# Two-layer cross attention: layer 2's image scores copied out of the score tile and sent through DRAM, in place of a product of their own

## The chip, the cores and the metric

The kernel runs on one core of a Trainium2 chip. The metric is the device time of one execution in microseconds (us); the median of several runs stands for a kernel. Beside the runs there is one profiled execution with its trace. Engines are named as in the profile: PE (TensorE matmuls), PEld (its weight loads), DVE (VectorE), ACT (ScalarE), POOL (GpSimd) and SP (SyncE, which issues most of the transfers here).

## What is computed

Two layers of cross attention with an image adapter, on 4096 tokens: x is 16 x 256 x 320, the context 16 x 256 x 512, with 20 heads of 16. The last 4 of the 256 context tokens of a batch are image tokens. Layer 2, the one that the change touches, cut to what matters (the output product and the residual follow):

```python
text_ehs, ip_ehs = encoder_hidden_states[:, :-4], encoder_hidden_states[:, -4:]
q, k_t, v_t = heads(hidden_states @ W_q), heads(text_ehs @ W_k), heads(text_ehs @ W_v)
probs_t = softmax(einsum('bhsd,bhtd->bhst', q, k_t) * attn_scale)
text_out = einsum('bhst,bhtd->bhsd', probs_t, v_t)
k_ip, v_ip = heads(ip_ehs @ W_k_ip), heads(ip_ehs @ W_v_ip)
attn_scores = einsum('bhsd,bhnd->bhsn', q, k_ip) * attn_scale
qsem = l2norm(einsum('bhst,bte->bhse', probs_t, text_ehs))
sem = einsum('bhse,bne->bhsn', qsem, l2norm(ip_ehs))
probs_ip = softmax(attn_scores + 0.5 * sem) * spatial_mask
out = text_out + einsum('bhsn,bhnd->bhsd', probs_ip, v_ip)
```

`attn_scores`, the scores of every query against the four image keys, are what the change gets in another way.

## The kernel before

The work is cut into slots: one slot is four heads (a group g of five) of one batch b. Slots 0 to 79 are layer 1, slots 80 to 159 layer 2, and two more drain the pipeline. Products that need full accuracy are made of rounded halves (a high and a low part). Queries, keys and activations are kept in DRAM (`qd`, `kd`, `x1d`) and come back as stacks (`qs`, `ks`) whose rows are the halves and, in layer 2, two rows with the row maxima.

A layer-2 slot k has two halves, t = 0 and 1, and each half of the tokens is one call of `both1` (L761). It issues, in this order:

- 4 matmuls into `T` (L775): transposed scores of slot k, already shifted by the row maxima;
- 4 matmuls into `S` (L780): plain scores of slot k + 2, 128 queries by 4 heads by 256 keys. S is one PSUM tile of two banks and has no second buffer. Its last four columns of each head (T1:S in the code) are the scores against the image keys; before, nothing reads them;
- DVE's maximum over the first 252 columns (L781), into `mn`;
- in the half t = 0, `attend1` of slot k - 2: 32 matmuls (L825, L828) into `P`;
- ACT's two exps of T into the tile P (L788).

Between the halves stand the other steps of the slot: `rounded1` (ACT's `ctb`, L806, and POOL's rest, L807), `norm1` of the slot before (L816 matmuls with the matrix `gm` into one X bank, four or three blocks, then DVE's multiply `wt`, L817, which frees the bank), and `maxima1` (L794: two small matmuls that turn `mn` into rows in an X bank, ACT's copy `mt`, L796, and a transfer from ACT's queue into `qs`). There are three X banks, used in turn by everything that isn't S, T or P. Fillers run at the thirds of a slot, from a table of due times: the next batch's keys (`kst`, `kd`), tokens (`gm`, `v1t`, `cta`), queries (L517 to L537), the image softmax (L881), and the batch's end (L931 the image output, L932 its add into `hT`, L754 the output rows `xc`).

The next batch's queries are `open1` (L942). After `queries` it calls `image1` (L502), two DVE multiplies (L506) which spread the four image keys over 128 columns with the mask `kmask`; nine matmuls (L205) of queries by these, into an X bank; and a DVE transpose (L955) into `si`, 128 x 8 x 32, the layout of the image softmax: the token in partitions and free dimension, then group and image key. The image softmax reads `si` on POOL (L899), one batch after.

PE's instructions keep the order of the program text. In the main loop the order of DVE, ACT, POOL and SP is chosen by the compiler's scheduler from its own timeline; `anchor` marks an instruction for others to be queued behind. SP issues the transfers in its order, and an issue that has to wait holds back those behind it.

Of the kernel before, what the change touches and what calls it, by code (L numbers as in the profile page):

```python
# [8 lines left out]
F32 = mybir.dt.float32  # L9
FR = mybir.dt.float32r  # L10
# [7 lines left out]
S = 256  # L18
# [6 lines left out]
NIP = 4  # L25
BI = B * NIP
T1 = S - NIP
# [21 lines left out]
def xattn2(  # L49
# [234 lines left out]

    rn = const_tile([128, BI], "rn")
    kip = const_tile([128, 2, 3, BI], "kip", FR)
    kmask = const_tile([128, 3, 32], "kmask")


    def keys_out(d, m, kst, b=slice(None)):  # L290
# [119 lines left out]
    def weights6():  # L410
        cip = w1["cip"]
        w1["v"] = yield from weights(wv1_d, "wC", None, 0.3, "rawc")
        wvi1 = yield from weights_by_column(wvi1_d, 0.3, "rawc")
        vip = buf("rawc", [128, 512], bufs=2, name="vip")[:BI, :CP]
        for m in range(3):
            ms = slice(m * 128, m * 128 + 128)
            vp = bank()[:BI, :128]
            prod(vp, lambda s, k: cip[:, s, k], lambda s, k: wvi1(s, k, ms), 4)
            nc.vector.tensor_copy(vip[:, ms], vp)
            yield  # L420
        ind1 = buf("M", [2, 2, S], FR, bufs=SIZES["M"], name="ind")
        nc.scalar.activation(ind1, ident[:2, :2].unsqueeze(2).to_broadcast([2, 2, S]), AF.Copy, scale=-1.0)
        w1["ind"] = ind1
        dma(kmask, kmask_d.rearrange("(m p) c -> p m c", p=128))
        dma(vipd, vip)
        for i in range(2):
            v = buf("wD", [128, 2, 640], bufs=2, name="v1t")
            nc.gpsimd.memset(v, 0.0)
            nc.vector.memset(vcols(v, V1W)[:, 0, :, 16], 1.0)
            nc.vector.tensor_scalar_add(vcols(v, V1W)[:, 1, :, 16], vcols(v, V1W)[:, 1, :, 16], tmask[:, 2:3])  # L430
            v1t.append(v)
        yield
# [35 lines left out]
    def tokens1(b):  # L468
# [29 lines left out]
                )  # L498
            yield
        return V, G  # L500

    def image1(b):  # L502

        kb = buf("kb", [128, 2, 3, 32, NIP], FR)
        for s in range(2):
            nc.vector.tensor_mul(  # L506
                kb[:, s],
                f(kip[:, s, :, 4 * b : 4 * b + 4]).unsqueeze(2).to_broadcast([128, 3, 32, NIP]),
                kmask.unsqueeze(3).to_broadcast([128, 3, 32, NIP]),
            )  # L510
        return kb.rearrange("p s m c n -> p s m (c n)")

    def split(src, neg, eng, tag):

# [113 lines left out]
    def stacks1(k):  # L628
        b, g = divmod(k - NS, NG)
        n = 2 * SIZES["NR"]  # L630
        i = ((NS - SIZES["NR"]) % SIZES["NR"]) * 2 + (k - NS) % n
        Q, K = QK[k] = [x[i // 2 % SIZES["NR"]][:, 2 * (i % 2) : 2 * (i % 2) + 2] for x in (qs, ks)]
        get("k1", b)
        qd = get("o1", b)[0]
        for u in range(2):
            rows = slice(64 * u, 64 * u + XROW)
            hs = slice(4 * g + u, 4 * g + u + 3, 2)
            if k - NS < n:
                dma(K[64 * u + XROW : 64 * u + KS1], w1["ind"])
            dma(K[rows], stack_rows(kd[1][b][:, :, 0])[:, hs])  # L640
            dma(Q[rows], stack_rows(qd)[:, hs])
# [101 lines left out]
    def finish(l, b, hT, resid, extra=None):  # L743
# [14 lines left out]
        yield from project(l, wo[l], hh, evac)  # L758
        return y

    def both1(k, t, between=None):  # L761

        a = k + 2 < 2 * NS and QK[k + 2] 
        c = NS <= k < 2 * NS and QK[k]
        if a:
            if t == 0:
                maxes[k + 2] = buf("mn", [128, 4, 4], FR, bufs=2)[:, :2]
            sp = scores()
        if c:
            st = [bank("T").rearrange("p (h t) -> p h t", h=2) for u in range(2)]  # L770
            lo = (0, DUP)[t]
            for j in range(2):
                for u in range(2):
                    rows = slice(64 * u, 64 * u + KS1)
                    mm(st[u][:, j], c[1][rows, j, lo : lo + 128], c[0][rows, j], start=True, stop=True)  # L775
        if a:
            for j in range(2):
                for u in range(2):
                    rows = slice(64 * u, 64 * u + XROW)
                    mm(sp[:, 2 * u + j], a[0][rows, j, t * 128 : (t + 1) * 128], a[1][rows, j], start=True, stop=True)  # L780
            anchor(nc.vector.tensor_reduce(maxes[k + 2][:, t], sp[:, :, :T1], axis=AX.X, op=ALU.max))  # L781
        if between:
            between()
        if c:
            for u in range(2):
                if t == 0:
                    P[k, u] = buf("P", [128, 2, 2, S], bufs=SIZES["NP"])
                anchor(nc.scalar.activation(P[k, u][:, t], st[u], AF.Exp, scale=SCALE))  # L788
# [92 lines left out]
    def image_softmax(b, lo=0, hi=NG):  # L881

        gs, n = slice(lo, hi), hi - lo
        nt, si = norms[b][:, gs], get("o1", b)[1]
        pool = nc.gpsimd
        small = lambda n, t: buf(t, [128, NG, 8] + ([n] if n > 1 else []))[:, gs]

# [54 lines left out]
    def open1(b):  # L942
# [4 lines left out]
        get("w2")  # L947
        qh, qd = yield from queries(1, xs)

        kb = image1(b)  # L950
        yield
        sp = bank()[:, :S]
        prod(sp, lambda s, k: kb[:, s, k], lambda s, k: qh[:, s, k], 3)
        si = buf("si", [128, 8, 32], bufs=3)
        nc.vector.transpose(si.rearrange("p f c -> p (f c)"), sp)  # L955
        yield
        return qd, si


    results, tasks, clock, delayed = {}, {}, [-99.0], []  # L960
# [224 lines left out]
```

## Time and profile before

| | |
|---|---|
| runs | 1620.82, 1624.44, 1625.23 us |
| median | 1624.44 us |
| span of the profiled execution | 1631.7 us |
| DVE busy | 1215.7 us, 75% |
| POOL busy | 1188.4 us, 73% |
| ACT busy | 828.8 us, 51% |

The profiled execution is 7.3 us longer than the median of the runs. Its busy times are sums over the whole program; layer 1 takes about the first 770 us of it, and layer 2 the rest. A row of a timeline has the start, the duration, the engine, the line and the operation, with what came out and what went in; idle time before it and its releaser stand in brackets. A row of a table of groups has the total, the mean of one in ns, and the idle time ahead of it. In a row of the table of windows, each engine has its busy time, then come the granted clock of PE, the share of time in which the DMA engines were busy, and GB/s.

### The profile page before, as it was taken

Reading aid. Unit: us, or ns where it says so; the run is one execution under the profiler, and the core shown is the slowest. Engines: PE = TensorE matmul, PEld = TensorE weight load, DVE = VectorE, ACT = ScalarE, POOL = GpSimd, SP = SyncE. Lnnn points to the kernel's source line nnn. Section 1 sums busy time; section 2 is a strip of 40 time slices with the busy share of each in tenths; the row PEclk is TensorE's granted clock in tenths of the full one; section 3 lists DMA queues with packets and bytes.
Section 4 is the critical chain, followed back from the end, with each engine's and each line's share of the span. In section 5 each row is a group of like instructions: output and inputs, shape, how many; then the busy total and the mean of one; then the engine's idle time right before and its main releaser. Section 6 shows DMA issues by size and latency. Waiting matters only on the chain.

```text
span 1631.7 us, 36363 instructions
## 1 busy us (share of the span) xinstructions
PE 1540.0 (94%) x13306; PEld 1235.5 (76%) x13306; DVE 1215.7 (75%) x2410; ACT 828.8 (51%) x1797; POOL 1188.4 (73%) x1147
## 2 busy tenths in 40 slices
PE   7899999999999899789999999999999999999996
PEld 6777878788878787577777777777777777777765
DVE  5467777677777677868877787878777887777785
ACT  5344545445454545435555555545554555555462
POOL 3358787878787867767688668766876787678776
PEclk9799999999999999799999999999999999999998
DMA  7767676667777675666424332433344243423301
GB/s 219 201 202 205 202 203 202 190 207 199 208 199 207 177 210 165 162 191 178 144 74 130 114 125 89 133 120 112 101 126 128 88 125 114 139 81 106 112 26 44
DMA packets 235741, 243.06 MB, mean 149 GB/s; under 512 B 19050, under 2 KB 219468, under 8 KB 235564
## 3 DMA queue, kind: packets, MB, share of 16 engines
q1 hardware_dynamic: 233356, 239.44, 49.8%
q8 instruction: 106, 1.74, 0.5%
q10 hardware_dynamic: 2208, 1.30, 0.3%
q14 instruction: 71, 0.58, 0.1%
HBM read 116.78 MB, written 88.18 MB: 126 GB/s over the span
## 4 chain that ended last, share of the span: by engine, by line
PE 55%; DVE 13%; DMA 10%; POOL 9%; ACT 4%; issue 3%; SPq 3%; ACTq 0%; POOLq 0%; DVEq 0%
PE X L205 15%; PE X L816 12%; PE X L528 7%; PE P L709 5%; PE P L825 3%; DMA qs<-mt 3%; POOL P L682 3%; PE S L652 3%; PE P L828 3%; DMA qs<-qd 3%; PE T L775 3%; SPq L82 2%; PE T L676 2%; DVE wt L817 2%; DVE ho L518 2%
## 5 line engine op out<-in xcount | busy, mean ns | idle before, releaser
L682 POOL TENSOR_TENSOR P<-P,rs 128x512 f32<-128x512 f32 x320 | 413.4, 1313 | 159.5 <-ACT P L679 159.2
L807 POOL TENSOR_TENSOR wt<-P,ctb 128x512 f32<-128x512 f32 x320 | 422.3, 1335 | 93.0 <-ACT ctb L806 91.3
L816 PE MATMUL X<-ctb,gm 128*128 128x512 f32 x1120 | 330.4, 413 | 2.1 <-DVE wt L817 1.1
L679 ACT ACTIVATE P<-T 128x512 f32<-128x512 f32 x320 | 176.1, 595 | 222.1 <-PE T L676 111.8
L806 ACT ACTIVATE ctb<-P 128x512 fp32r<-128x512 f32 x320 | 195.6, 631 | 98.3 <-PE X L816 91.5
L816 PEld LDWEIGHTS X<-ctb,gm 128*128 128x128 f32 x1120 | 189.2, 188 | 72.3 <-issue 15.6
L817 DVE TENSOR_TENSOR wt<-X,wt 128x512 f32<-128x512 f32 x320 | 218.2, 683 | 33.9 <-PE X L816 28.4
L781 DVE TENSOR_REDUCE mn<-S 128x4 fp32r<-128x1008 f32 x160 | 191.8, 1199 | 48.3 <-PE S L780 48.2
L788 ACT ACTIVATE P<-T 128x512 f32<-128x512 f32 x320 | 173.7, 595 | 64.3 <-PE P L825 48.3
L654 DVE TENSOR_REDUCE mn<-S 128x4 fp32r<-128x716 f32 x160 | 142.5, 891 | 0.0
L709 PE MATMUL P<-P,vr 128*32 128x256 f32 x1920 | 132.1, 409 | 3.3 <-DVE mx L581 2.3
L676 PE MATMUL T<-qs,ks 127*128 127x256 f32 x640 | 112.3, 295 | 22.6 <-DMA qs<-mt 10.7
L652 PE MATMUL S<-ks,qs 125*128 125x256 f32 x640 | 118.4, 309 | 3.7 <-DVE mn L654 2.5
L652 PEld LDWEIGHTS S<-ks,qs 125*128 125x128 f32 x640 | 89.3, 196 | 40.6 <-issue 35.0
L528 PE MATMUL X<-ho,wF 128*128 128x256 f32 x768 | 112.8, 290 | 6.3 <-DVE ho L518 3.0
L528 PE MATMUL X<-hq,wE 128*128 128x256 f32 x768 | 111.5, 289 | 7.1 <-ACT hq L517 3.3
L894 POOL TENSOR_TENSOR r<-u,rs 128x40 f32<-128x40 f32 (+2 forms) x17 | 108.7, 6393 | 7.7 <-DVE u L891 7.6
L676 PEld LDWEIGHTS T<-qs,ks 127*128 127x128 f32 x640 | 92.8, 198 | 28.0 <-DVE tmp L726 11.6
L528 PEld LDWEIGHTS X<-ho,wF 128*128 128x128 f32 x768 | 103.2, 194 | 12.6 <-DVE ho L518 4.7
L528 PEld LDWEIGHTS X<-hq,wE 128*128 128x128 f32 x768 | 103.5, 195 | 11.7 <-ACT hq L517 3.7
L205 PE MATMUL X<-cta,wA 128*128 128x252 f32 (+1 forms) x720 | 100.9, 286 | 7.3 <-ACT wA L147 5.7
L205 PEld LDWEIGHTS X<-cta,wA 128*128 128x128 f32 x720 | 94.1, 195 | 12.5 <-ACT wA L147 5.9
(197 smaller groups left out, 2813.6 us busy)
## 6 DMA issues: line engine op xcount, KB each, us to landing
qd<-q SPq DMA_DIRECT2D x96, 384.0 KB
qs<-tph SPq DMA_DIRECT2D x64, 308.0 KB
kd<-kst SPq DMA_DIRECT2D x73, 256.0 KB
rawc<-in_cT_dram SPq DMA_DIRECT2D x60, 256.0 KB
qs<-qd SPq DMA_DIRECT2D x80, 192.0 KB
ks<-kd SPq DMA_DIRECT2D x80, 192.0 KB
ks<-kd SPq DMA_DIRECT2D x160, 96.0 KB
qs<-qd SPq DMA_DIRECT2D x160, 96.0 KB
```

Of the source, the lines that this page charges most:

```text
L205: last = mm(out, lhs(a, k), rhs(b, k), start=i == 0, stop=i == len(terms) - 1)
L528: mm(pp, w(s, k, slice(m * 128, (m + 1) * 128)), a[:, t], start=i == 0, stop=i == len(terms) - 1)
L652: mm(sp[:, h], Q[: XROW + T0, h, t * 128 : (t + 1) * 128], K[: XROW + T0, h], start=True, stop=True)
L676: mm(st[p][:, j], K[:KS0, 2 * p + j, t * 128 : (t + 1) * 128], Q[:KS0, 2 * p + j], start=True, stop=True)
L679: exp = anchor(nc.scalar.activation(pt, st[p], AF.Exp, scale=SCALE))
L682: anchor(nc.gpsimd.tensor_mul(pt, pt, rs[:, t : t + 1].to_broadcast([128, 2, S])))
L709: mm(pv[32 * s : 32 * s + 32, o : o + S], v[:, vt, h : h + 32], P[k, s // 2][:, t, s % 2], start=vt < 2, stop=vt != 1,)
L781: anchor(nc.vector.tensor_reduce(maxes[k + 2][:, t], sp[:, :, :T1], axis=AX.X, op=ALU.max))
L806: nc.scalar.activation(R[k, u][:, t], P[k, u][:, t], AF.Copy, scale=0.5)
L807: anchor(nc.gpsimd.tensor_sub(W[k, u][:, t], P[k, u][:, t], f(R[k, u][:, t])))
L816: mm(yp, gm[:, gb], R[k, u][:, kt], start=i == 0, stop=i == len(blocks[n]) - 1)
L817: nc.vector.tensor_mul(W[k, u][:, n], yp, W[k, u][:, n])
```

## The change

The product is taken out, with `image1`, `kmask` and the transpose. `both1` calls a new function, `image_scores`, after the S matmuls and ahead of the maximum. It copies the four image columns of each head out of S on ACT, into a tile `sq` (two buffers) which collects the five groups and both halves of a batch; that is 160 copies of 128 x 16. After the batch's last copy one transfer stores `sq` to DRAM (`sd`, two buffers), and eight transfers load it as `si`, now 128 x 8 x 20, each into 32 partitions, 4 x 20 numbers in each, in runs of 20 numbers. All nine go on SP's queue, 144 in all. `open1` gives `qd` alone, and the softmax takes `si` from `image[b]`.

```diff
-    kmask = const_tile([128, 3, 32], "kmask")
...
-        dma(kmask, kmask_d.rearrange("(m p) c -> p m c", p=128))
...
-    def image1(b):
-
-        kb = buf("kb", [128, 2, 3, 32, NIP], FR)
-        for s in range(2):
-            nc.vector.tensor_mul(
-                kb[:, s],
-                f(kip[:, s, :, 4 * b : 4 * b + 4]).unsqueeze(2).to_broadcast([128, 3, 32, NIP]),
-                kmask.unsqueeze(3).to_broadcast([128, 3, 32, NIP]),
-            )
-        return kb.rearrange("p s m c n -> p s m (c n)")
...
-        qd = get("o1", b)[0]
+        qd = get("o1", b)
...
+    image = {}
+
+    def image_scores(k, t, sp):
+
+        b, g = divmod(k - NS, NG)
+        if (g, t) == (0, 0):
+            image[b] = buf("sq", [128, 2, 4, NG * NIP], bufs=2)
+        sq = image[b]
+        split_heads = lambda x: x.rearrange("p (u j) n -> p j u n", u=2)
+        nc.scalar.copy(
+            sq[:, t, :, NIP * g : NIP * (g + 1)].rearrange("p (j u) n -> p j u n", u=2), split_heads(sp[:, :, T1:S])
+        )
+        if (g, t) == (NG - 1, 1):
+            sd = dram.tile([128, 2, 4, NG * NIP], F32, tag="sd", name="sd", bufs=2)
+            dma(sd, sq)
+            si = image[b] = buf("si", [128, 8, NG * NIP], bufs=3)
+            for s in range(4):
+                for u in range(2):
+                    dma(si[32 * s : 32 * s + 32, 4 * u : 4 * u + 4], sd[:, u, s].rearrange("(a r) x -> r a x", r=32))
...
+            image_scores(k + 2, t, sp)
             anchor(nc.vector.tensor_reduce(maxes[k + 2][:, t], sp[:, :, :T1], axis=AX.X, op=ALU.max))
...
-        nt, si = norms[b][:, gs], get("o1", b)[1]
+        nt, si = norms[b][:, gs], image[b]
...
-        kb = image1(b)
-        yield
-        sp = bank()[:, :S]
-        prod(sp, lambda s, k: kb[:, s, k], lambda s, k: qh[:, s, k], 3)
-        si = buf("si", [128, 8, 32], bufs=3)
-        nc.vector.transpose(si.rearrange("p f c -> p (f c)"), sp)
-        yield
-        return qd, si
+        return qd
```

PE's order is the same but for the 144 matmuls that are gone. On the other engines the scheduler sets the order anew; three places follow, each in the slot of a batch in which ACT also casts the next queries (`hq`), in the half t = 1, with what each instruction waits for in brackets. In the changed kernel the line numbers are others: L789 is the maximum, L757 the copy, L796 the exps, L814 `ctb`, L825 `wt`, L504 and L506 the cast and the fix of `hq`.

ACT before, from the last `gm` cast of the half to `ctb` of the slot:

```order
L485 CAST gm<-X 128x124
L788 ACTIVATE P_92<-T 128x512 [waits PE_49]
L788 ACTIVATE P_93<-T 128x512 [waits PE_49]
L517 CAST hq_276<-xq_120 128x768
L806 ACTIVATE ctb_81<-P_92 128x512 [waits Activation_49,Pool_49]
```

ACT in the changed kernel, the same stretch:

```order
L483 CAST gm<-X 128x124
L796 ACTIVATE P_92<-T 128x512 [waits PE_49]
L796 ACTIVATE P_93<-T 128x512 [waits PE_49]
L504 CAST hq_275<-xq_120 128x768
L757 COPY sq_9283<-S 128x4x4 [waits PE_49]
L814 ACTIVATE ctb_81<-P_92 128x512 [waits Activation_49,Pool_49]
```

The copy out of S stands behind both exps and the cast. In the half t = 0 of a slot it stands ahead of the exps.

DVE before, from the fix of `gm` to the second `wt` behind the maximum:

```order
L486 TENSOR_TENSOR gm<-X,gm 128x128 [waits Activation_49]
L902 TENSOR_REDUCE m_0_10450<-a_10376 128x40 [waits Pool_49]
L781 TENSOR_REDUCE mn_532<-S 128x4 [waits PE_49]
L817 TENSOR_TENSOR wt<-X,wt 128x512 [waits PE_49]
L519 SCALAR_TENSOR_TENSOR hq_276<-hq_276,tmask,xq_120 128x256 [waits Activation_49]
L909 TENSOR_REDUCE z_0_10506<-a_10376 128x40 [waits Activation_49]
L489 SCALAR_TENSOR_TENSOR v1t<-X,tmask,rn 128x20x4 [waits PE_49]
L910 RECIPROCAL z_0_10506<-z_0_10506 128x40 [waits DVE_49]
L817 TENSOR_TENSOR wt<-X,wt 128x512 [waits PE_49]
```

DVE in the changed kernel:

```order
L910 TENSOR_REDUCE m_0_10440<-a_10365 128x40 [waits Pool_49]
L484 TENSOR_TENSOR gm<-X,gm 128x128 [waits Activation_49]
L825 TENSOR_TENSOR wt<-X,wt 128x512 [waits PE_49]
L789 TENSOR_REDUCE mn_531<-S 128x4 [waits Activation_49]
L506 SCALAR_TENSOR_TENSOR hq_275<-hq_275,tmask,xq_120 128x256 [waits DMAHW2_49]
L487 SCALAR_TENSOR_TENSOR v1t<-X,tmask,rn 128x20x4 [waits PE_49]
L917 TENSOR_REDUCE z_0_10507<-a_10365 128x40 [waits Activation_49]
L825 TENSOR_TENSOR wt<-X,wt 128x512 [waits PE_49]
```

The maximum waits for ACT instead of PE, as do all 160 of layer 2, and a `wt` has moved ahead of it in this slot. In the slot with the `xc` rows the order of DVE is the same as before.

SP in the changed kernel, from the store of the batch's scores on:

```order
L82 DMA sd<-sq_9283 128x160 [waits DMAHW6_49,Activation_49]
L82 DMA si_9778<-sd 32x4x20 [waits DMAHW7_49,DMAHW6_49]
L82 DMA si_9778<-sd 32x4x20 [waits DMAHW0_49]
...
L82 DMA out_dram<-xc_676 128x3x256 [waits DVE_49]
L82 DMA si_9778<-sd 32x4x20 [waits DMAHW7_49]
L82 DMA xq_120<-x1d 128x3x256 [waits DMAHW0_49,Pool_49]
...
L82 DMA xc_676<-x1d 128x3x256 [waits DMAHW6_49,DMAHW3_49]
L82 DMA rawc_88<-in_cT_dram 128x2x256 [waits DMAHW4_49,Pool_49]
```

The store and five of the loads stand ahead of the batch's `out_dram`, the other three between it and the `xc` load; before, `out_dram`, `xq`, `xc` and `rawc` followed each other.

## The prediction, made before the changed kernel had run

> **What bounds the kernel now.** I read the page first, then the table of windows for the stretch in which only layer 2 runs (770 to 1548 us of the span), then the list of what PE waited for in it, then the timeline of one batch of layer 2, slot by slot. The page names PE; the window row gives PE 767.92 of 778.00 us at a granted clock of 1.00, and next come DVE 610.54, POOL 574.20 and ACT 422.41:
>
> ```profile
> PE 1540.0 (94%) x13306; PEld 1235.5 (76%) x13306; DVE 1215.7 (75%) x2410; ACT 828.8 (51%) x1797; POOL 1188.4 (73%) x1147
> ```
>
> ```profile
> 770.00:1548.00 778.00, 767.92 (x6608) 591.03 (x6610) 610.54 (x1107) 422.41 (x884) 574.20 (x547) 1.00 0.37 114
> ```
>
> ```profile
> PE X L931 <- DVE wt L817: 6.5, 12, 0.6
> ```
>
> So layer 2 is a stream of matmuls with almost no gap: 778.00 - 767.92 = 10.1 us idle in 778, and the largest listed wait is 6.5 us for a DVE multiply. Two things follow. A matmul taken off PE is worth its whole time, and a new wait of PE is paid in full too, because there is no idle time for it to fall into. DVE, at 78%, is not full, but PE's X banks (a ring of three) come free only by DVE's multiplies (`wt`), so DVE's position in its order is what can stop PE.
>
> **Part 1, removed: the product.** Per batch nine matmuls leave PE, and two multiplies and a transpose leave DVE. The chain of waits has the product on the path, in the middle of a batch:
>
> ```profile
> 1247.49 0.12 PE X L794 x2
> 1247.61 1.12 PE X L205 x9
> 1248.73 0.44 PE T L775 x4
> ```
>
> ```profile
> L506 DVE TENSOR_TENSOR kb<-kip,kmask 128x384 fp32r<-128x384 f32 x26 | 28.6, 1098 | 5.0 <-PE X L205 5.0
> ...
> L205 PE MATMUL X<-q,kb 128*128 128x256 f32 x126 | 18.0, 287 | 0.1
> ```
>
> From 1247.61 to the next T matmul at 1248.73 is 1.12 us; by the group's 287 ns for one it would be 9 x 0.287 = 2.6, but matmuls overlap and their ends are modelled, so I take the step in the chain, rounded up for a second batch in which the same step took 1.20 us: 1.20. Sixteen batches: 16 x 1.20 = 19.2 us off PE. On DVE 2 x 1.098 us of multiplies go and a transpose, some 2.6 us of a batch, which is not on the path by itself. One X bank use per batch goes as well.
>
> **Part 2, added: the copies, 160 on ACT, and the gate they make.** No ACT copy of 128 x 16 from this tile is in the trace. The nearest rows are a cast of 128 x 64 and a copy of 128 x 77:
>
> ```profile
> L576 ACT COPY sp<-X 128x77 f32<-128x77 f32 x32 | 6.5, 235 | 4.6 <-PE X L574 4.6
> ...
> L147 ACT CAST kip<-X 128x64 fp32r<-128x64 f32 x3 | 0.6, 205 | 1.6 <-PE X L205 1.6
> ```
>
> Both have more elements, at 205 and 235 ns, so 0.235 us bounds the copy from above and nothing from below; I take 0.20, by the nearer row. 160 x 0.20 = 32 us on an engine that is busy 422 of 778 us is nothing by itself. What matters is where the copy stands. In the changed order every layer-2 row-maximum reduce on DVE waits for ACT, where before it waited for PE; both read the tile S. The reduce therefore cannot start at S's end but after the copy, and in a half with t=1 ACT has the two exps of the half ahead of the copy.
>
> The Trainium skill, page "PSUM — Partial Sum Buffer", section "PSUM bank collisions raise a hardware error", says that two engines may not touch the same bank and 32-partition quadrant at once, reads against reads included, so the copy and the reduce have to take turns and the wait cannot simply be dropped. By this rule the sum is the one below; without turns it would be part 1 alone. No run of before shows it, since S has one reader there.
>
> I price it slot type by slot type; a batch has five, each with one t=1 half and one t=0 half. First a t=1 half, that of the slot with the `xc` evacuation:
>
> ```profile
> 1255.13 0.40 PE L780 MATMUL S<-ks,qs 48*128 48x256 f32 x4
> 1255.33 1.09 ACT L788 ACTIVATE P<-T 128x512 f32<-128x512 f32 x2 [0.17 <-PE T L775]
> ...
> 1255.58 1.21 DVE L781 TENSOR_REDUCE mn<-S 128x4 fp32r<-128x1008 f32 x1
> ...
> 1257.66 0.48 DVE L754 SCALAR_TENSOR_TENSOR xc<-X,bo,xc 128x256 f32<-128x256 f32 x1 [0.27 <-PE X L528]
> ...
> 1258.28 0.95 PE L205 MATMUL X<-wC,cta 128*128 128x320 f32 x5
> 1258.36 0.69 DVE L817 TENSOR_TENSOR wt<-X,wt 128x512 f32<-128x512 f32 x1 [0.21 <-PE X L816]
> ```
>
> S ends at 1255.53 and the reduce starts at 1255.58. The exps end at 1256.42; a copy right behind them ends at about 1256.50 (consecutive ACT instructions overlap by 0.1 us), so the reduce starts at about 1256.54, 0.96 us late. Behind it on DVE stand a `wt` multiply, `xc` and another `wt`. The reduce takes 1.12 us of the queue, the multiply then starts at 1257.66, `xc` at 1258.27 and ends at 1258.75; it frees the X bank for the L205 group, which started at 1258.28 and now can at 1258.81: **+0.53**. Second, the slot in which ACT also casts `hq`:
>
> ```profile
> 1266.31 0.40 PE L780 MATMUL S<-ks,qs 48*128 48x256 f32 x4
> ...
> 1266.52 1.10 ACT L788 ACTIVATE P<-T 128x512 f32<-128x512 f32 x2
> ...
> 1267.17 1.20 DVE L781 TENSOR_REDUCE mn<-S 128x4 fp32r<-128x1008 f32 x1
> ...
> 1267.49 0.85 ACT L517 CAST hq<-xq 128x768 fp32r<-128x768 f32 x1
> ...
> 1268.88 0.47 DVE L519 SCALAR_TENSOR_TENSOR hq<-hq,tmask,xq 128x256 fp32r<-128x256 f32 x1
> ...
> 1269.51 0.30 DVE L489 SCALAR_TENSOR_TENSOR v1t<-X,tmask,rn 128x80 f32<-128x80 f32 x1
> ...
> 1269.89 1.16 PE L528 MATMUL X<-ho,wF 128*128 128x256 f32 x8
> ```
>
> Now the copy stands behind the cast too (1267.49 + 0.85 = 1268.34, copy to 1268.42). The reduce goes from 1267.17 to 1268.46. In the new order the `wt` multiply comes ahead of it, `hq` and `v1t` behind it: the reduce is done at 1269.66, `hq` at 1270.05, `v1t` at 1270.27, and the L528 group that needs the bank `v1t` frees moves from 1269.89 to 1270.31: **+0.42**. Third, the slot with the product itself:
>
> ```profile
> 1244.32 0.40 PE L780 MATMUL S<-ks,qs 48*128 48x256 f32 x4
> ...
> 1244.77 1.21 DVE L781 TENSOR_REDUCE mn<-S 128x4 fp32r<-128x1008 f32 x1
> ...
> 1245.95 0.69 DVE L817 TENSOR_TENSOR wt<-X,wt 128x512 f32<-128x512 f32 x1
> ...
> 1247.33 0.28 PE L794 MATMUL X<-ident_r,mn 128*4 128x128 f32 x2
> ```
>
> The reduce starts 0.95 late, the multiply behind it ends at 1247.59 instead of 1246.64; the small matmuls of `maxima1` need its bank and stood at 1247.33, so 0.69 of the delay is covered: **+0.25**. Fourth, the slot with the image output (L931), where a `cta` cast precedes the copy:
>
> ```profile
> 1272.55 1.05 PE L828 MATMUL P<-wt,zone 128*32 128x256 f32 x16
> ...
> 1276.64 0.40 PE L780 MATMUL S<-ks,qs 48*128 48x256 f32 x4
> ...
> 1277.74 1.20 DVE L781 TENSOR_REDUCE mn<-S 128x4 fp32r<-128x1008 f32 x1
> ...
> 1277.81 0.62 ACT L147 CAST cta<-rawc 128x512 fp32r<-128x512 f32 x1
> ...
> 1278.86 0.68 DVE L817 TENSOR_TENSOR wt<-X,wt 128x512 f32<-128x512 f32 x1
> ...
> 1279.46 1.29 DVE L932 TENSOR_TENSOR hT<-hT,X 128x256 f32<-128x256 f32 x3
> ...
> 1279.94 1.05 PE L816 MATMUL X<-ctb,gm 128*128 128x512 f32 x3
> ```
>
> Here DVE was late itself (reduce at 1277.74). The cast ends at 1278.43, so the copy ends at 1278.5, and the reduce runs from 1278.81 behind a multiply that now precedes it; the first `hT` add ends at 1280.36, and the L816 group that follows its bank moves from 1279.94 to 1280.40: **+0.46**. Fifth:
>
> ```profile
> 1287.14 0.40 PE L780 MATMUL S<-ks,qs 48*128 48x256 f32 x4
> ...
> 1288.91 1.20 DVE L781 TENSOR_REDUCE mn<-S 128x4 fp32r<-128x1008 f32 x1
> ```
>
> The reduce starts 1.37 us after S's end for other reasons, later than the copy's 0.97: **0**. In the t=0 halves the copy stands ahead of the exps, so the reduce is only 0.2 to 0.25 us late, and the attend matmuls cover it: in the first row of the fence before last the second sixteen of them run from 1272.55 for 1.05 us, and they take no bank that this reduce holds up. If that cover were gone, the price would be 5 x 0.25 = 1.25 us per batch. The sum is 0.25 + 0.53 + 0.42 + 0.46 + 0 = 1.66 us per batch; 16 x 1.66 = 26.6 us.
>
> **Part 3, added: nine transfers per batch on SP's queue.** One store of `sq` to DRAM and eight loads `si` at some 0.4 us an issue: 9 x 0.41 = 3.7 us. SP is mostly empty there:
>
> ```profile
> 1203.83 0.43 SPq L82 DMA_DIRECT2D qs<-qd  x1
> 1217.29 0.40 SPq L82 DMA_DIRECT2D out_dram<-xc  x1
> 1219.52 0.38 SPq L82 DMA_DIRECT2D xq<-x1d  x1
> ```
>
> ```profile
> 1211.23 0.40 PE L780 MATMUL S<-ks,qs 48*128 48x256 f32 x4
> ```
>
> It sits from 1204.26 to 1217.29 with nothing but the `out_dram` store's wait for `xc`. The batch's last S (1211.23, a batch ahead of the one at 1266.31, so a batch is 55.1 us) ends at 1211.63, its copy a little after 1212, so the store and five loads (6 x 0.41 = 2.5 us) go out in the 5 us left, if the store lands within some 2.5 us; three loads come between `out_dram`, `xq` and `xc` and shift them by about 1.2. What stands behind them, `xq`, is cast only in the next batch (ACT's `hq` at 1267.49), the stacks are loaded four slots of 11 us ahead, and `si` is used in the next batch's image softmax. I take 0: below, a transfer put ahead of others cannot hurry them; above, 3.7 us per batch if all of the issues reached PE.
>
> **Sum.** Against the profiled execution's span of 1631.7: -19.2 + 26.6 + 0 = +7.4. The median of the three runs is 7.3 below that span, so by the runs 1624.4 + 7.4, about **1632 us**. Bounds of the gate: nothing at the bottom (all of it is absorbed by DVE's 22% idle time), 5 x 0.96 = 4.8 us per batch at the top (every late reduce reaches PE whole).
>
> **The rivals.**
>
> *The gate is absorbed; pure saving.* DVE loses 2.6 us of work per batch and has about 12 us of idle time in it. If the X banks are freed early enough, only part 1 is left: 1624.4 - 19.2 = 1605. For it: the largest listed wait on DVE is 6.5 us in 778, so usually the banks are free in time. Against it: in four of five slot types above, the instruction that frees the bank ends within 0.1 to 0.7 us of the matmul that takes it.
>
> *DVE falls behind.* Each delay of about 0.96 reaches PE whole, since the reduce also gates `maxima1`, the `mt` transfer into the stacks and the next S (one buffer). Then 5 x 0.96 - 1.20 = 3.6 us per batch, x 16 = 58; with the fifth slot at nothing (3.84 - 1.20) x 16 = 42. I take the middle: 1624 + 50 = 1674. It decides where the slack before the L794 and L205 groups is under 0.1 us. Against it: I found 0.69 us in one slot type and a DVE that was itself late in another.
>
> *SP's queue.* The store's landing holds the eight loads, and these the `out_dram`, `xq` and `xc` behind them. From a landing of more than some 2.5 us on, the time beyond moves these. If all 3.7 us of the issues reached PE it would be 16 x 3.7 = 59 us; the slack of a batch speaks against it, so I take a quarter, 15 us on top of the forecast: 1647.
>
> **How the numbers follow.** Forecast 0.57, pure saving 0.26, DVE behind 0.13, SP's queue 0.04. The least difference that a measurement of this kernel can tell from nothing is about 0.3%, 4.9 us, so faster ends at 1619.6 and slower begins at 1629.3. The forecast's own range, is 1619 to 1645: below, a copy of no length takes 0.2 us out of each of the four slots (16 x 0.8 = 13 us); above, the 0.69 us of cover in the third slot is gone (16 x 0.69 = 11 us) and the copy takes 0.235. The larger part lies above 1629.3: 0.39 slower, 0.17 within, 0.01 faster. With the rivals: faster 0.26 + 0.01 = 0.27, same 0.17, slower 0.39 + 0.13 + 0.04 = 0.56. The range for 8 in 10 reaches down over the pure saving and leaves out DVE behind: 1603 to 1652.
>
> **What would show it.** In the timeline of the changed kernel a layer-2 reduce at t=1 starts about 1.0 us after S's end, with the copy as its releaser; if it starts at 0.05 the gate is no gate. PE's idle time in a stretch of 14 batches goes from 10 us to about 33 (10 + 14 x 1.66); near 10 the rival of the pure saving holds, above 60 DVE is behind. The waits of PE name DVE's `xc`, `v1t`, `hT` and `wt`, at the four places above, each 0.2 to 0.5 us. The product's group is gone. If SP's `xq` or `xc` loads are waited for by anyone but SP, part 3 is wrong. The forecast falls if the copy takes far more or less than 0.2 us, or if ACT's order differs from the one read here.

## The result and the profile after

The changed kernel takes as long as the kernel before: 1625.89 us median (1621.32 to 1628.91, 12 runs) against 1625.53 us (1620.82 to 1629.81, 12 runs), a ratio of 0.9998 with a 95% interval of 0.9985 to 1.001. The profiled execution of the changed kernel has a span of 1623.6 us.

From the page of the changed kernel, busy time and share of the span by engine, and the group of the maxima:

```profile
PE 1519.2 (94%) x13162; PEld 1220.3 (75%) x13162; DVE 1181.5 (73%) x2362; ACT 844.2 (52%) x1957; POOL 1179.8 (73%) x1147
...
L789 DVE TENSOR_REDUCE mn<-S 128x4 fp32r<-128x1008 f32 x160 | 192.1, 1201 | 89.8 <-ACT sq L757 88.9
```

PE does 1540.0 - 1519.2 = 20.8 us less, as a kernel without 144 matmuls should, and the time is the same: what was taken off came back as waiting. The 160 copies took 0.18 us each:

```profile
L757 ACT COPY sq<-S 128x16 f32<-128x16 f32 x160 | 28.2, 176 | 33.2 <-PE S L787 16.6 <-PE P L833 16.2 <-issue 0.2
```

The window of layer 2 (us, then busy time and instructions by engine, the granted clock, the DMA share and GB/s) and the list of PE's waits in it say so too:

```profile
770.00:1548.00 778.00, 757.01 (x6518) 579.42 (x6517) 584.56 (x1069) 437.48 (x1029) 570.90 (x550) 1.00 0.39 117
```

```profile
PE X L824 <- DVE wt L825: 12.1, 12, 1.0
PE X L802 <- DVE mn L789: 3.2, 3, 2.2
PE X L939 <- DVE mn L789: 1.9, 1, 1.9
```

PE is idle for 778.00 - 757.01 = 21.0 us instead of 10.1. The maxima (L789, now released by ACT's copy `sq`, with 88.9 us of idle time on DVE before them against 48.2 before) are late, as forecast, but the long waits stand at places that I hadn't named: twelve waits of up to 1.0 us in the last slot of a batch, and a few of about 2 us and more near the start of layer 2.

PE's instructions stand in one order in all the kernels of this study, except for the product's (and a small one added in e6_bank_kept). So each matmul of one trace can be set beside the same matmul of another. The next table is made that way, against the profiled execution of the kernel before: how many us longer each slot of layer 2 takes, as means over slots 90 to 149 by the five slots of a batch (named by what they hold: the product, the `xc` rows, the `hq` cast, the image output, and the last), their sum per batch, and the totals over slots 80 to 89, 90 to 149 and 150 to the end. What lies before slot 80 is not in it; layer 1 differs by some us between traces, and what of this belongs to the change stands under the second experiment. The rows below the first two are the experiments of the next section.

```
kernel               product     xc     hq  image   last   batch   80-89  90-149   150-
predicted              -0.95   0.53   0.42   0.46   0.00    0.46
changed                -1.13   0.05   0.01  -0.63   0.99   -0.70    14.5    -8.4    1.2
e1_copies_only          0.22   0.52   0.00   0.42   0.11    1.27     7.6    15.2    3.4
e2_no_product          -1.14  -0.02   0.01  -0.04  -0.01   -1.20    -1.5   -14.4   -1.4
e3_vb_behind           -1.13   0.05   0.01  -0.61   0.42   -1.25     7.2   -15.1   -0.5
e4_copy_behind         -1.15  -0.02   0.01  -0.19   0.14   -1.20    -2.4   -14.4   -1.2
e5_both                -1.15  -0.02   0.01   0.11  -0.25   -1.29    -2.2   -15.5   -0.8
e6_bank_kept           -0.75   0.22   0.01   0.38   0.11   -0.02    14.8    -0.3    1.7
e7_order_of_before     -1.12   0.05   0.02   0.33  -0.25   -0.98     8.7   -11.8    0.9
e8_wt_first            -1.14  -0.02   0.01   0.34  -0.24   -1.05    -0.9   -12.6    0.8
```

In its steady part the changed kernel does gain, 0.70 us per batch, 8.4 us over twelve batches. It loses 14.5 us in the first ten slots of layer 2. From 735 to 850 us its list of PE's waits begins with the maxima:

```profile
PE X L802 <- DVE mn L789: 10.7, 5, 6.7
```

Four places in its timeline show how. First, the half with the `xc` rows, on which I had put 0.53 us:

```profile
1247.96 0.40 PE L787 MATMUL S<-ks,qs 48*128 48x256 f32 x4
1248.15 1.09 ACT L796 ACTIVATE P<-T 128x512 f32<-128x512 f32 x2 [0.17 <-PE T L782]
...
1249.12 0.18 ACT L757 COPY sq<-S 128x16 f32<-128x16 f32 x1
...
1249.34 1.21 DVE L789 TENSOR_REDUCE mn<-S 128x4 fp32r<-128x1008 f32 x1 [0.92 <-ACT sq L757]
...
1251.06 0.47 DVE L741 SCALAR_TENSOR_TENSOR xc<-X,bo,xc 128x256 f32<-128x256 f32 x1
1251.10 1.09 PE L205 MATMUL X<-wC,cta 128*128 128x320 f32 x6
```

The step up to the maximum came out as written: S ends at 1248.36, the copy starts right behind the exps, 0.76 us later, and the maximum starts 0.98 us after S's end (forecast 1.0). But L205 starts at 1251.10 while `xc` still runs, to 1251.53, with no wait. It does not take the bank that `xc` frees.

Second, the start of layer 2, on DVE, ACT, SP and PE:

```profile
747.30 0.38 SPq L82 DMA_DIRECT2D nt<-in_bmask_dram  x1
...
748.62 0.18 ACT L757 COPY sq<-S 128x16 f32<-128x16 f32 x1
...
750.32 0.77 DVE L930 TENSOR_TENSOR rs<-rs,nt 128x384 f32<-128x384 f32 x1 [3.97 <-DMA nt<-in_bmask_dram]
...
754.69 1.19 DVE L789 TENSOR_REDUCE mn<-S 128x4 fp32r<-128x1008 f32 x1
...
755.93 0.27 PE L802 MATMUL X<-ident_r,mn 128*4 128x128 f32 x1 [6.66 <-DVE mn L789]
```

`rs<-rs,nt` is the multiply of a batch's image values by their mask (`vb` and `bmask` in the code, one per batch). The scheduler put it ahead of a maximum, and it stood there for 3.97 us until the mask's load, issued at 747.30, had landed. The maximum behind it came 5.9 us after its copy, and PE waited 6.66 us. In the profile before, the same multiply waited 0.7 us for the load and PE not at all.

Third, three slots later, ACT:

```profile
791.73 0.51 ACT L147 CAST wF<-rawc 128x384 fp32r<-128x384 f32 x1 [1.89 <-DMA rawc<-in_wo_dram]
792.15 0.17 ACT L757 COPY sq<-S 128x16 f32<-128x16 f32 x1
...
792.35 1.21 DVE L789 TENSOR_REDUCE mn<-S 128x4 fp32r<-128x1008 f32 x1 [1.87 <-ACT sq L757]
...
793.61 0.22 PE L802 MATMUL X<-ident_r,mn 128*4 128x128 f32 x1 [2.22 <-DVE mn L789]
```

ACT works in order here. Its cast of a weight waited 1.89 us for a load, the copy stood behind it, though its S had ended at 788.56, the maximum behind the copy, and PE waited 2.22 us. From 750 to 860 us of the profile before, the list of PE's waits holds a single entry, 0.9 us for POOL's `hq`.

Fourth, the last slot of a batch:

```profile
1275.10 1.04 DVE L930 TENSOR_TENSOR rs<-rs,nt 128x384 f32<-128x384 f32 x1 [0.64 <-DMA rs<-vipd]
...
1278.16 1.19 DVE L789 TENSOR_REDUCE mn<-S 128x4 fp32r<-128x1008 f32 x1
```

```profile
1280.19 0.67 DVE L825 TENSOR_TENSOR wt<-X,wt 128x512 f32<-128x512 f32 x1
...
1280.92 1.19 PE L824 MATMUL X<-ctb,gm 128*128 128x512 f32 x4 [1.01 <-DVE wt L825]
```

The same multiply stands ahead of `ho` here, waits 0.64 us for its load, and takes 1.04 us. Before the change it stood behind the maximum and took 0.54 us:

```profile
1284.71 1.20 DVE L781 TENSOR_REDUCE mn<-S 128x4 fp32r<-128x1008 f32 x1
1285.82 0.54 DVE L922 TENSOR_TENSOR rs<-rs,nt 128x384 f32<-128x384 f32 x1
```

The means over all 16 batches, before and after, are 545 and 898 ns:

```profile
L922 DVE TENSOR_TENSOR rs<-rs,nt 128x384 f32<-128x384 f32 x16 | 8.7, 545 | 0.8 <-DMA nt<-in_bmask_dram 0.7
```

```profile
L930 DVE TENSOR_TENSOR rs<-rs,nt 128x384 f32<-128x384 f32 x16 | 14.4, 898 | 13.5 <-DMA rs<-vipd 9.6 <-DMA nt<-in_bmask_dram 4.0
```

DVE reaches the `wt` that L824 waits for about 1 us late.

### The profile page after: what moved, and what is told of

It is laid out like the page before. It is cut to its first block, busy times and chain, and to the rows that moved or that the text cites. A ratio compares the mean times of both kernels' runs of the same rounds, so it can differ in the third digit from the quotient of the medians.

```text
span 1623.6 us, 36382 instructions
## 1 busy us (share of the span) xinstructions
PE 1519.2 (94%) x13162; PEld 1220.3 (75%) x13162; DVE 1181.5 (73%) x2362; ACT 844.2 (52%) x1957; POOL 1179.8 (73%) x1147
## 2 busy tenths in 40 slices
DMA packets 256078, 245.64 MB, mean 151 GB/s; under 512 B 37338, under 2 KB 239804, under 8 KB 255900
## 4 chain that ended last, share of the span: by engine, by line
PE 70%; DMA 10%; DVE 10%; ACT 3%; POOL 2%; SPq 2%; issue 2%; ACTq 0%; POOLq 0%; DVEq 0%
PE X L205 18%; PE X L824 14%; PE X L515 9%; PE P L696 6%; PE S L639 4%; PE P L833 4%; PE T L782 3%; PE P L836 3%; PE T L663 3%; DMA qs<-qd 2%; DMA rs<-vipd 2%; DVE ho L505 2%; DMA kd<-kst 2%; PE S L787 2%; SPq L82 2%
## 5 line engine op out<-in xcount | busy, mean ns | idle before, releaser
L815 POOL TENSOR_TENSOR wt<-P,ctb 128x512 f32<-128x512 f32 x320 | 414.6, 1314 | 87.2 <-ACT ctb L814 86.2
L824 PE MATMUL X<-ctb,gm 128*128 128x512 f32 x1120 | 330.2, 413 | 12.8 <-DVE wt L825 12.1
L789 DVE TENSOR_REDUCE mn<-S 128x4 fp32r<-128x1008 f32 x160 | 192.1, 1201 | 89.8 <-ACT sq L757 88.9
L825 DVE TENSOR_TENSOR wt<-X,wt 128x512 f32<-128x512 f32 x320 | 218.5, 684 | 48.6 <-PE X L824 43.5
L824 PEld LDWEIGHTS X<-ctb,gm 128*128 128x128 f32 x1120 | 189.8, 188 | 81.7 <-issue 20.2
L814 ACT ACTIVATE ctb<-P 128x512 fp32r<-128x512 f32 x320 | 196.6, 635 | 88.4 <-PE X L824 54.8
L796 ACT ACTIVATE P<-T 128x512 f32<-128x512 f32 x320 | 173.8, 597 | 34.8 <-PE T L782 13.4
L515 PE MATMUL X<-ho,wF 128*128 128x256 f32 x768 | 113.4, 291 | 7.1 <-DVE ho L505 3.2
L515 PE MATMUL X<-hq,wE 128*128 128x256 f32 x768 | 110.8, 288 | 8.0 <-ACT hq L504 3.4
L515 PEld LDWEIGHTS X<-ho,wF 128*128 128x128 f32 x768 | 103.9, 195 | 13.0 <-DVE ho L505 5.1
L515 PEld LDWEIGHTS X<-hq,wE 128*128 128x128 f32 x768 | 103.0, 194 | 12.9 <-ACT hq L504 3.9
L205 PE MATMUL X<-cta,wA 128*128 128x252 f32 (+1 forms) x720 | 101.2, 288 | 8.1 <-ACT wA L147 6.1
L205 PEld LDWEIGHTS X<-cta,wA 128*128 128x128 f32 x720 | 94.8, 196 | 14.3 <-ACT wA L147 6.4
```

The source lines that it names most:

```text
L205: last = mm(out, lhs(a, k), rhs(b, k), start=i == 0, stop=i == len(terms) - 1)
L515: mm(pp, w(s, k, slice(m * 128, (m + 1) * 128)), a[:, t], start=i == 0, stop=i == len(terms) - 1)
L814: nc.scalar.activation(R[k, u][:, t], P[k, u][:, t], AF.Copy, scale=0.5)
L815: anchor(nc.gpsimd.tensor_sub(W[k, u][:, t], P[k, u][:, t], f(R[k, u][:, t])))
L824: mm(yp, gm[:, gb], R[k, u][:, kt], start=i == 0, stop=i == len(blocks[n]) - 1)
L825: nc.vector.tensor_mul(W[k, u][:, n], yp, W[k, u][:, n])
```

## The experiments

The first four runs were to tell where the cost sits: in the lateness of the maxima itself (theory "gate", the one on record), in the order that the scheduler chooses once the copy is there (theory "order"), or nowhere, because the product had been worth nothing. The kernel before had a median of 1625.45 us beside them.

**Copies alone** (e1_copies_only). Before, with this in `both1`, ahead of the maximum, and no transfers:

```diff
+            image_scores(k + 2, t, sp)
             anchor(nc.vector.tensor_reduce(maxes[k + 2][:, t], sp[:, :, :T1], axis=AX.X, op=ALU.max))
```

> The kernel before with the 160 copies out of S alone (into a tile that nothing reads), the product kept and no transfers. Theory 'order': the copies ahead of the maxima make the scheduler put other DVE work first (a wt multiply ahead of the maximum, the multiply of the image values by their mask, rs<-rs,nt, ahead of ho), and this order with the late maxima costs what the product saves, about 19 us: 1645 us. Theory 'gate' (as predicted: each late maximum is paid by PE, 1.66 us per batch): 1652 us. Theory 'the product was worth nothing': 1626 us, since the copies then cost nothing either.

Measured: 1652.53 us, ratio 1.0158 (1.0142 to 1.0174), 27.1 us more. This is the gate, with the order that the scheduler makes of it, and without the product's removal. Three slots cost what I had priced them at, 0.22, 0.52 and 0.42 us where I had 0.25, 0.53 and 0.46; the `hq` slot (0.42 forecast) shows nothing. So a batch pays 1.27 us in place of 1.66, and the total meets the forecast of 26.6 us only because the first ten slots pay 7.6 us, where two batches at 1.66 would be 3.3. The half with `xc`, in which PE's weight load shows the wait:

```profile
1265.17 0.40 PE L793 MATMUL S<-ks,qs 48*128 48x256 f32 x4
...
1266.55 1.21 DVE L795 TENSOR_REDUCE mn<-S 128x4 fp32r<-128x1008 f32 x1 [0.92 <-ACT sq L770]
...
1268.27 0.48 DVE L754 SCALAR_TENSOR_TENSOR xc<-X,bo,xc 128x256 f32<-128x256 f32 x1
...
1268.80 0.45 PEld L205 LDWEIGHTS X<-wC,cta 128*128 128x128 f32 x3 [0.30 <-DVE xc L754]
```

S ends at 1265.57; the maximum, `xc` and L205 follow 0.98, 2.70 and 3.23 us after. In the changed kernel `xc` follows at the same 2.70 and L205 at 2.74. So DVE is equally late in both, and what differs is which bank L205 takes. The scheduler's order in this kernel is that of the changed kernel in the image and last slots too (`wt` ahead of the maximum, `rs<-rs,nt` ahead of `ho`), yet it loses 0.42 us in the image slot where the changed kernel gains 0.63. Order alone cannot be the answer.

**No product** (e2_no_product). Before, with the product, its multiplies and its transpose left out:

```diff
-        kb = image1(b)
         yield
-        sp = bank()[:, :S]
-        prod(sp, lambda s, k: kb[:, s, k], lambda s, k: qh[:, s, k], 3)
-        si = buf("si", [128, 8, 32], bufs=3)
-        nc.vector.transpose(si.rearrange("p f c -> p (f c)"), sp)
+        si = buf("si", [128, 8, 32])
+        if b == 0:
+            nc.gpsimd.memset(si, 0.0)
```

> The kernel before without the product, its two multiplies and its transpose; the image scores are a tile of zeros, so the image tokens' scores are left out of the output. Theories 'order' and 'gate': the product is on PE's path, 16 x 1.2 = 19 us less, 1606 us. Theory 'the product was worth nothing': 1626 us.

Measured: 1603.37 us, ratio 0.9858 (0.9838 to 0.9878), 22.1 us less. The product's slot gains 1.14 us, the other four nothing, 1.20 per batch. So the product did lie on PE's path, and the changed kernel gives all of its worth back.

The slots of layer 2 make up 17.3 us of this (1.5 + 14.4 + 1.4). The traces show where the rest lies: in layer 1, where the queries of layer 2's first batch are made. Set beside the kernel before, the ten slots 60 to 69 are 5.9 to 7.0 us shorter in each of the eight kernels without the product, and 1.5 us in e1_copies_only, which keeps it. Before:

```profile
650.87 2.33 DVE L506 TENSOR_TENSOR kb<-kip,kmask 128x384 fp32r<-128x384 f32 x2
...
656.11 0.41 DVE L726 TENSOR_TENSOR tmp<-nt,P 128x256 f32<-128x256 f32 x1
...
656.57 0.80 PE L676 MATMUL T<-qs,ks 127*128 127x256 f32 x2 [3.87 <-DVE tmp L726]
```

In the changed kernel:

```profile
645.40 0.42 DVE L713 TENSOR_TENSOR tmp<-nt,P 128x256 f32<-128x256 f32 x1
...
646.02 1.05 PE L663 MATMUL T<-qs,ks 127*128 127x256 f32 x4
```

Before, the product's two multiplies (`kb`, 2.33 us) stand on DVE ahead of `tmp`, with a weight's multiply of 1.50 us that the scheduler also puts there, and PE waits 3.87 us for `tmp`. Without the product both are gone from that place, and these matmuls don't wait. No run separates the two.

**The image values' multiply tied down** (e3_vb_behind). The changed kernel with

```diff
-        nc.vector.tensor_mul(vb, vb, w1["bmask"])
+        queued(nc.vector.tensor_mul(vb, vb, w1["bmask"]))
```

> The changed kernel with one DVE instruction tied down: the multiply of the image values by their mask (rs<-rs,nt) is queued behind the maximum that precedes it in the program, so that it can stand neither at the start of layer 2, where it waits 4 us for the mask's load, nor ahead of ho in the last slot of a batch. Theory 'order': the 6.6 us at the start and the 1.0 us per batch go, 6.6 + 15 x 1.0 = 22 us, about 1604 us. Theory 'gate': the maxima still wait for the copies, 1626 us.

Measured: 1608.07 us, ratio 0.9889 (0.9872 to 0.9907), 17.4 us less than before. One instruction's place on DVE holds most of the loss: the second slot of layer 2 is 6.4 us shorter than in the changed kernel, and the last slot of each batch 0.57 us. The waits of PE in 850 to 1540 us:

```profile
PE X L824 <- DVE wt L825: 6.3, 12, 0.5
```

The twelve waits shrank from 12.1 to 6.3 us. I had expected the whole 1.0 us of the last slot to go; half of it stayed.

**The copy behind the maximum** (e4_copy_behind). The changed kernel with two lines exchanged:

```diff
-            image_scores(k + 2, t, sp)
             anchor(nc.vector.tensor_reduce(maxes[k + 2][:, t], sp[:, :, :T1], axis=AX.X, op=ALU.max))
+            image_scores(k + 2, t, sp)
```

> The changed kernel with the copy issued behind the maximum instead of ahead of it, so the maximum waits for PE as before and ACT's copy waits for DVE. Theory 'order' and theory 'gate': both costs go with the place of the copy, and the product's 19 us are left: 1606 us. If the cost lies in the nine transfers per batch instead: 1626 us.

Measured: 1601.87 us, ratio 0.9847 (0.9828 to 0.9865), 23.6 us less than before: faster than both kernels. ACT's copy now waits for DVE, the list of PE's waits from 850 to 1540 us doesn't name the copy, and the scheduler's order of DVE goes back to that of before at the end of a batch, but for a few instructions elsewhere. It does the same 160 copies and 144 transfers as the changed kernel and is as fast as the kernel with no copies, no transfers and no product (1603.37), so copies and transfers cost nothing by themselves that these runs can tell. Where the copy stands is worth 24 us: 23.6 here, and the 0.4 that the changed kernel was above before. What is left of PE's waits from 850 to 1540 us is short:

```profile
PE X L939 <- DVE wt L825: 4.9, 12, 0.4
PE X L824 <- DVE wt L825: 3.8, 12, 0.3
```
The Trainium skill, page "PSUM — Partial Sum Buffer", section "PSUM bank collisions raise a hardware error", which the prediction weighed, says that two engines may not touch one bank and 32-partition quadrant at once, reads against reads included. In the traces they do take turns: the maximum waits for the copy in the changed kernel, the copy for the maximum here. No run lets them overlap. Which of them goes first is what these runs price, at 24 us.

The next four stand beside a median of 1626.04 us for the kernel before. The compiled programs suggest a further theory, "banks". PSUM tiles T and X are not dealt out in turn, as I had written of the X banks: the program's planner places each one in a bank of its own choice, in layer 2 mostly over banks 2 to 7, and a kernel with other uses or another order can get another placement. For two halves, by kernel, in order of use:

```
half with xc      wt  L528(xc)  wt  maxima1  L205
before            2   4         3   2        4
e1_copies_only    2   4         3   2        4
e2_no_product     3   4         5   2        3
e4_copy_behind    3   4         5   2        3
changed           3   4         5   2        6
e6_bank_kept      2   4         5   2        3

half with image   wt  L931      wt  maxima1
before            2   3 4 2     3   4
e1_copies_only    2   3 4 2     3   4
e2_no_product     2   3 4 2     3   4
e4_copy_behind    2   3 4 2     3   4
changed           3   5 7 2     3   4
e6_bank_kept      2   3 4 2     3   4
```

In the first, L205 takes bank 4 behind `xc` in the kernel before, and bank 6 in the changed kernel. In the second, the last `wt` group takes bank 3 behind the first image matmul, which the `hT` add frees after the late maximum; in the changed kernel it takes it behind the first `wt`, which DVE does ahead of the maximum. In the half with `xc` the product's removal is enough to move L205 off the bank that `xc` frees (e2, e4); in the half with the image output it is not, and the placement moves only where the copy also stands ahead of the maximum.

**A bank use kept** (e6_bank_kept). The changed kernel with a small matmul where the product was:

```diff
+        yield
+        sp = bank()[:, :S]
+        mm(sp, qh[:, 0, 0, :128], qh[:, 0, 0], start=True, stop=True)
+        si = buf("si_x", [128, 8, 32])
+        nc.vector.transpose(si.rearrange("p f c -> p (f c)"), sp)
+        yield
         return qd
```

> The changed kernel with one matmul of 128x256 into an X bank and one transpose out of it per batch, where the product stood; nothing reads the result. Theory 'banks': PSUM tiles are placed anew when the product's bank use goes, and this moved the late multiplies away from the matmuls that I priced; with a bank use kept, the tiles of the image output's slot and of the product's slot lie as before, so these two slots lose about 0.45 and 0.2 us per batch against the kernel before, in place of -0.6 and 0, while the xc slot stays at 0 because its L205 lies in another bank here: with 0.15 for the matmul about 1.4 us per batch above the changed kernel, 1626 + 21 = 1647 us. Theory 'order': DVE's order is that of the changed kernel, so only the matmul's 0.15 comes on top, 1628 us, and the slots show 0 and -0.6.

Measured: 1633.93 us, ratio 1.0046 (1.0031 to 1.0061). The total lies between the two expectations, 7.9 us above the kernel before; the slots are clearer. The image slot loses 0.38 us as with the copies alone, in place of a gain of 0.63, with DVE's order the same but for three instructions, and the list of waits from 850 to 1540 us names the add that the placement predicts:

```profile
PE X L824 <- DVE hT L940: 8.9, 12, 0.7
```

With the copies alone, where the placement of this half is the same, it is the same wait:

```profile
PE X L830 <- DVE hT L946: 8.9, 12, 0.7
```

The product's slot is at -0.75, which is -1.14 and 0.15 for the small matmul and about 0.2 for the gate. Two points of the expectation failed: the `xc` slot lost 0.22 where I expected nothing, and the last slot only 0.11 where I left it at 1.0. The second is why 1647 us was too high. Image and last slot go together: over both, the changed kernel loses 0.99 - 0.63 = 0.36 us and this one 0.49. It looks as if PE waited in the one for what it had gained in the other; no run here tests that alone.

**Order of before, gate kept** (e7_order_of_before). The changed kernel with `wt` and the image values' multiply queued behind the maximum:

```diff
-        nc.vector.tensor_mul(W[k, u][:, n], yp, W[k, u][:, n])
+        queued(nc.vector.tensor_mul(W[k, u][:, n], yp, W[k, u][:, n]))
...
-        nc.vector.tensor_mul(vb, vb, w1["bmask"])
+        queued(nc.vector.tensor_mul(vb, vb, w1["bmask"]))
```

> The changed kernel with every wt multiply and the image values' multiply queued behind the maximum that precedes them in the program, so DVE's order in the halves t = 1 is that of before, and the maxima still wait for the copies. Theory 'gate': the late maximum now delays wt, and the image output's L931 waits for it, +0.8 us in that slot in place of -0.6, while the last slot's cost goes: about 1608 + 15 x (1.4 - 0.45) = 1622 us. Theory 'order alone' (the lateness costs nothing where the order is that of before): 1602 us, as with the copy behind.

Measured: 1613.70 us, ratio 0.9923 (0.99 to 0.9946), between the two theories: 11.8 us above the copy behind the maximum. The image slot goes to +0.33 (expected +0.8), the last one to -0.25. In the half with the image output DVE's order is that of before and the placement is that of the changed kernel (3, 5 7 2, 3, 4); elsewhere the ties move more instructions than the expectation says, so this is not the whole order of before. Most of the 11.8 us is in the first ten slots (8.7 against -2.4), where PE waits for late maxima, once 2.58 us behind a copy that stands behind a cast that waited 2.25 us for a load. So with an order near that of before the lateness still costs, but it costs at the start of layer 2 and 0.2 us per batch after it.

**Both** (e5_both). The copy behind the maximum, and the image values' multiply queued as above.

> The changed kernel with the copy behind the maximum and with the image values' multiply queued behind the maximum ahead of it, both. Theory 'order': with the copy behind, the scheduler already leaves that multiply behind, so nothing more is to be had: 1602 us, as with the copy behind alone. If the multiply costs something there too: down to 1598 us.

Measured: 1602.78 us, ratio 0.9859 (0.9839 to 0.9878), no different from the copy behind the maximum alone, as "order" expected.

**`wt` first** (e8_wt_first). The same, and in the slot with the image output the maximum is put behind the `wt` multiply that PE waits for:

```diff
+                inst = nc.vector.tensor_reduce(maxes[k + 2][:, t], sp[:, :, :T1], axis=AX.X, op=ALU.max)
+                anchor(queued(inst, *behind) if behind else inst)
...
-            yield lambda: norm1(last, 1, 0)
+            yield lambda: late.append(norm1(last, 1, 0)) if defer else norm1(last, 1, 0)
+            if defer:
+                yield lambda: late.pop(0)(late.pop(0))
```

> The kernel with the copy behind the maximum and the image values' multiply tied, and in the slot with the image output also the maximum put behind the wt multiply that PE's L931 waits for. If the 0.6 us gained there by the changed kernel came from this place of wt: 15 x 0.45 = 7 us less, 1595 us. If the hT add behind the later maximum then holds PE's next bank: no gain, 1602 us.

Measured: 1607.81 us, ratio 0.9887 (0.9869 to 0.9905), 5 us worse than without. The image slot loses 0.34 us. PE's waits from 850 to 1540 us:

```profile
PE X L833 <- DVE hT L952: 9.9, 13, 0.9
```

The wait for `wt` went, and the `hT` add behind the later maximum took its place, the second of the two expectations and somewhat worse. In the kernels with the copy behind, the bank of the next group is the one that this add frees. The changed kernel's gain of 0.63 us there needed both the order and its placement: with its order and the placement of before the slot loses (0.38 in e6_bank_kept), and with its placement and the order of before too (0.33 in e7_order_of_before).

## Why the prediction was right and where it was wrong

The range (1603 to 1652 us) held the time, 1625.9. The direction did not come: slower by 7.4 us was forecast, and the change is 0.4 us, inside what can be told from nothing, to which the prediction gave 0.17.

**What bounds the kernel:** right. A matmul off PE was worth its time, and a new wait was paid: the 1.01 us at L824 is 0.99 us in its slot. PE's idle time in the window, for which 33 us had been named, came to 21.0.

**Part 1, the product:** 19.2 us forecast, 22.1 measured (19.8 to 26.3 by the interval); the 1.20 us per batch of layer 2 is exact. The rest lies in layer 1. The prediction put the product's work on DVE at nothing ("not on the path by itself"), having read one batch in the middle of layer 2; at the first batch PE waited 3.87 us behind it and a weight's multiply. By the following account this is the term that turned slower into the same. In the slots of layer 2 the changed kernel is 14.5 - 8.4 + 1.2 = 7.3 us longer than the kernel before, and about 5 us of that come back in slots 60 to 69 (6.4 us shorter, against 1.5 with the product kept). The remaining 2 us are within what layer 1 differs by.

**Part 2, the gate:** as a total, 26.6 us forecast against 24 for the place of the copy (and 27.1 with the product kept). As a mechanism up to the maximum, right to some hundredths of a us. Its way on to PE was wrong in two steps. The prediction said that the X banks are "a ring of three" and read from a timeline of the kernel before which instruction frees the bank of which matmul. That holds with the product kept, for three of five slots; the changed kernel has another placement, and then the steps for the `xc` slot (+0.53, measured 0.05), the product's slot (+0.25, measured about 0) and the image slot (+0.46, measured -0.63) fall. In the `hq` slot (+0.42, measured 0.01, also with the product kept) L528 started 0.08 us after `v1t` had ended, and I took that nearness for a wait; its row has no releaser in brackets. In the changed kernel the maximum came as late as forecast, and the same matmuls (L515) start ahead of `v1t`:

```profile
1261.29 1.20 DVE L789 TENSOR_REDUCE mn<-S 128x4 fp32r<-128x1008 f32 x1
...
1262.72 1.16 PE L515 MATMUL X<-ho,wF 128*128 128x256 f32 x8
...
1263.30 0.29 DVE L487 SCALAR_TENSOR_TENSOR v1t<-X,tmask,rn 128x80 f32<-128x80 f32 x1
```

And the fifth slot, put at nothing, pays 0.99 us. The steady gate is 1.20 - 0.70 = 0.5 us per batch instead of 1.66.

What was left out made up for it: the start of layer 2, at 14.5 us against -1.5 without product and copies. Two mechanisms were seen there. The multiply of the image values, moved ahead of a maximum, waits for its mask's load (e3 takes 6.4 us off by tying it); and copies behind ACT's casts inherit their waits for loads, which is read from the timeline (2.22 us) and was not taken away alone. I had read the new orders in the middle of layer 2 only, and the forecast of one average batch times sixteen had no place for events that occur once. That the total of the gate came out near was a coincidence of these two errors, and so was 7.3 us in layer 2 against the forecast's 7.4; that the range held the time is luck to this extent.

**Part 3, the transfers:** right, 0. With 160 copies and 144 transfers the kernel with the copy behind is as fast as the one without any.

**The rivals.** The pure saving (1605) is what the two lines in the other order give, 1601.9; the prediction gave it to DVE's idle time absorbing the wait, which is not how it comes about. DVE falling behind and SP's queue did not occur as such.

## What to carry to other kernels

When a second reader is added to a PSUM tile, put the small, late one behind the reader that the critical path needs: these two lines, exchanged, were worth 24 us of 1626. A new wait also changes what a scheduler puts first, so read its order at the places that occur once (first loads, a stage's start) and not only in the repeated middle; this holds for work that is taken away as well. Which instruction frees the bank that a matmul takes is to be read from the placement in the changed program, since a change of tiles and order can move the others; an end that is close to a start in a timeline is not yet a wait.

## What was not expected of the hardware

ACT's copy of 128 x 16 out of PSUM took 0.18 us; the bound from wider rows had been 0.235. A DVE multiply of 128 x 384 took 0.90 us on the mean of 16 in the places where the changed kernel put it, against 0.55 us before; why is not settled. The 128 loads in runs of 80 bytes, with which the packets under 512 bytes rise from 19050 to 37338 on the page, left no mark on the time (1601.87 us with them and the copy behind, 1603.37 without product, copies and transfers).
